# The last steps of a graph-attention layer on one core: products and selections placed earlier, row stores on two queues, scores by pairs with GpSimd

## The chip, the cores and the metric

One core of a Trainium2 chip. It has TensorE (PE), VectorE (DVE), ScalarE (ACT), GpSimd (POOL) and SyncE (SP), which only issues transfers here; ACT and POOL issue transfers too. The metric is the device time of one execution in microseconds (us), as the median of several. A "profiled execution" is one more execution, recorded by the hardware profiler: its span and all durations below come from it.

## The reference

A layer of attention over the edges of a graph, in front of it a layer norm and a relu, behind it a residual. There are N = 12,500 nodes of F = 128 features and E = 212,500 edges, sorted by the node `dst` that they end at; 8 heads of 16 features.

```python
h = jnp.maximum(_layernorm(x), 0.0)
q = (h @ Wq.T + bq).reshape(N, 8, 16)
k = (edge_h @ Wk.T + bk).reshape(-1, 8, 16)
v = (h @ Wv.T + bv).reshape(N, 8, 16)
qs, qd = q[src], q[dst]
in_m, out_m, diag_m = sum(qs * k), sum(qd * k), sum(qs * qd)   # over the 16 features
score = (softmax_of_dst(in_m / 4) + softmax_of_dst(out_m / 4)
         + softmax_of_dst(diag_m / 4)) * distance ** lam
h = segment_sum(score[..., None] * v[dst], dst, N).reshape(N, 128)
return x + leaky_relu(h @ Wo.T + bo, 0.1)
```

Since `v[dst]` is one row for all edges of a node, the last sum is v times one score per node and head: for each of the three softmaxes the kernel needs, per node and head, the sum of exp(logit) and the sum of exp(logit) times distance. Those are 24 + 24 numbers per node, called sums.

## The kernel before, in words

**Blocks and turns.** The edges are cut into blocks of 512. Five streams (S = 5) of 84 blocks (T = 84, G = 83) go side by side: step `g` of the loop handles stream `g % 5`, turn `t = g // 5`. There are 415 steps. In one step POOL issues four indirect transfers that gather q of the edges' sources (L683), PE transposes the edge rows and multiplies them by Wk (L1212, L1219, L1221) and spreads q of the ends (L1229), ACT builds one-hot matrices and copies out of PSUM (L1206, L1207, L1214, L1232), and DVE makes three products and a reduction to the logits (L1240 to L1243).

**Behind the logits**, a turn or two later, one call per step for all five streams: `turn_logits` transposes the logits into a PSUM tile `l_ps` (L1263); `scan_here` or, in the last turns, `scan_on` runs a maximum along the edges of a node forwards (L1321, with a short scan back over the block's head, L1326), and `scan_back` backwards (L1333); `turn_max` transposes that into `m_ps` (L1345); `powers` subtracts it on DVE (L1353) and takes the exponential on ACT (L1354, for the short piece behind the last turn L1358); `weigh_powers` multiplies by the distance's power (L1365). `select` loads the ends of the edges (L1371), `show_ends` compares them on PE into `d_ps` (L1379) and ACT makes 0/1 matrices of that (L1382, L1383). `to_rows` multiplies powers by these matrices into `w_ps` (L1393), 16 products a turn, copied by ACT (L1398), and `put_rows` stores the rows in DRAM as `sums`, five stores a turn (L1409); their places are register values, loaded into SP's registers once a turn (L654). The piece behind the last turn is called turn G (83) and has 16 partitions.

**Nodes.** Nodes are handled in units of 256 rows and pairs of units (class `Nodes`): load x and sums, normalise, multiply by Wv (`project_v`, bias L1150 and product L1152, into a PSUM tile that `weigh` reads), `scores` (L1094 to L1100: the two halves of the sums added, bounded below, a reciprocal, a product, two additions), `weigh` (v times score, L1160), `turn` (transposes L1144, ACT's copy L1147), `project_o` (bias L1150, product with Wo L1152, ACT's scaling by 0.1, L1171), `add_x` (the leaky relu's maximum, L1176, and the addition of x, L1177), `store` (L1183; the last part of the last unit L1185). Most pairs pass inside the loop, once their sums are complete. The pair called `leaving` has its product in the last turn; `last_pair` comes behind it; nine units are left to the end, as five pairs `rest[0]` to `rest[4]` (the last a single unit). Each of `rest`'s units has sums from one stream or from two; two parts are added (L1696). `hold(rest[r], name)` computes v of such a pair ahead and leaves it in a PSUM tile of that name.

**Order.** Each engine runs its instructions in the order of the program: every instruction is passed to `pin`, which chains it behind the last one of its engine. So a wait of one instruction holds all behind it on that engine. The PSUM tiles `l_ps`, `m_ps`, `d_ps`, `w_ps` and `node_ps` share three buffers (function `small`), handed out in the order of the program: a fourth waits until all readers of the first are done. `eT_ps` has one buffer, `k_ps` and `qd_ps` two each, shared with the loop.

Behind the loop the order was: the rest of turn 80's stores, logits and scans of turns 81 to 83, `powers` for all three, `weigh_powers` for all three, then `to_rows` and `put_rows` turn by turn; then the loads of all sums, the remaining `hold` products, the last pair's end, and the nine rest units:

```python
for r in range(len(rest) + 2):
    if r < len(rest):
        rest[r].weigh(rest[r].held)
    if 0 <= r - 1 < len(rest):
        rest[r - 1].turn(small([P, JN, P], "node_ps"))
    if 0 <= r - 2:
        rest[r - 2].project_o(small([P, JN, F], "node_ps"))
        rest[r - 2].add_x(nc.vector)
        rest[r - 2].store()
```

## Time and profile before

| what | value |
|---|---|
| median of 4 runs | 2201.59 us (2199.41 to 2204.81) |
| the profiled execution's own time | 2203.34 us |
| its span | 2201.5 us |
| instructions | 36,004 |
| busy PE, DVE, ACT, POOL | 1777.9, 2044.2, 1357.6, 1593.3 us |
| mean granted clock of PE | 0.792 |
| last gather issued by POOL (L683) | 2130.09 us |
| last reduction of logits on DVE (L1243) starts | 2135.81 us |
| last product of w_ps ends (L1393) | 2157.62 us |
| first load of the rest's sums on SP (L1125) | 2163.32 us |
| first weighing of a rest pair on DVE (L1160) | 2179.63 us |
| last store of the output issued (L1185) | 2195.08 us |

Times inside the execution count from the span's start. A row such as `L683 POOL DMA_INDIRECT qq<-q_table,src_i x1608 | 1526.7, 949 | 511.4` says: line 683, engine and operation, output and input tile, how often, then busy time, mean of one in ns, and the idle time in front of them. In a timeline a row is: start, duration, engine, line, operation, tiles and shapes, number of instructions run together, and in brackets how long the engine sat idle before it and what ended that. The granted clock says which share of its full clock PE was given: at 0.5 its instructions take twice as long.

### The profile page before, as it was taken

Reading aid. Unit: us, or ns where it says so; the run is one execution under the profiler, and the core shown is the slowest. Engines: PE = TensorE matmul, PEld = TensorE weight load, DVE = VectorE, ACT = ScalarE, POOL = GpSimd, SP = SyncE. Lnnn points to the kernel's source line nnn. Section 1 sums busy time; section 2 is a strip of 40 time slices with the busy share of each in tenths; the row PEclk is TensorE's granted clock in tenths of the full one; section 3 lists DMA queues with packets and bytes.
Section 4 is the critical chain, followed back from the end, with each engine's and each line's share of the span. In section 5 each row is a group of like instructions: output and inputs, shape, how many; then the busy total and the mean of one; then the engine's idle time right before and its main releaser. Section 6 shows DMA issues by size and latency. Waiting matters only on the chain.

```text
span 2201.5 us, 36004 instructions
## 1 busy us (share of the span) xinstructions
PE 1777.9 (81%) x10744; PEld 1415.4 (64%) x10744; DVE 2044.2 (93%) x2844; ACT 1357.6 (62%) x2518; POOL 1593.3 (72%) x1683
## 2 busy tenths in 40 slices
PE   6678788878888887887888887788887888778785
PEld 5556566656666666676676676666666677667664
DVE  7758999999999999999999999999999999999894
ACT  6665656656656665666566566566666566556561
POOL 7477777777777777777777777777777777777750
PEclk9766877887888888778778788787888787788776
DMA  7676554554555555545445545545545545544531
GB/s 213 202 227 176 178 159 149 180 170 149 184 161 163 153 180 184 162 145 183 150 145 176 163 147 161 170 143 161 173 140 176 163 144 167 161 152 142 160 95 58
DMA packets 321411, 355.63 MB, mean 162 GB/s; under 512 B 135267, under 2 KB 241006, under 8 KB 320897
## 3 DMA queue, kind: packets, MB, share of 16 engines
q1 hardware_dynamic: 250853, 237.91, 34.1%
q0 software_dynamic: 53184, 108.92, 17.3%
q10 hardware_dynamic: 17168, 6.41, 1.2%
q8 instruction: 87, 1.43, 0.3%
q14 instruction: 119, 0.97, 0.1%
HBM read 320.86 MB, written 32.17 MB: 160 GB/s over the span
## 4 chain that ended last, share of the span: by engine, by line
DVE 44%; PE 16%; DMA 13%; issue 4%; ACT 4%; POOL 2%; DVEq 1%; SPq 0%; ACTq 0%; POOLq 0%
DVE lT L1243 16%; DMA qq<-q_table,src_i 13%; DVE prod L1240 6%; DVE prod L1242 6%; DVE prod L1241 6%; PE k_ps L1221 4%; DVE m L1333 4%; PE w_ps L1393 3%; PE eT_ps L1212 3%; DVE l_ps L1303 2%; POOL qq L683 2%; PE k_ps L1219 1%; DVE back L1353 1%; PE m_ps L1345 1%; PE qd_ps L1229 1%
## 5 line engine op out<-in xcount | busy, mean ns | idle before, releaser
L683 POOL DMA_INDIRECT qq<-q_table,src_i x1608 | 1526.7, 949 | 511.4 <-issue 211.9
L1243 DVE TENSOR_REDUCE lT<-prod 128x96 f32<-128x1536 f32 x415 | 727.5, 1753 | 14.4
L1221 PEld LDWEIGHTS k_ps<-wk,eT 128*128 128x128 f32 x3320 | 502.8, 232 | 200.4 <-issue 200.4
L1221 PE MATMUL k_ps<-wk,eT 128*128 128x128 f32 x3320 | 594.1, 334 | 0.0
L1232 ACT COPY qd<-qd_ps 128x512 f32<-128x512 f32 x415 | 244.6, 589 | 153.3 <-DVE prod L1242 153.0
L1212 PE MATMUL eT_ps<-ident,ea 128*128 128x128 f32 x1660 | 312.0, 320 | 25.6 <-ACT eT L1214 24.6
L1354 ACT ACTIVATE back<-back 128x480 f32<-128x480 f32 x83 | 50.1, 604 | 423.3 <-DVE back L1353 417.9
L1206 ACT ACTIVATE relb<-relb,before 126x512 bf16<-126x512 bf16 x415 | 303.5, 731 | 0.0
L1240 DVE TENSOR_TENSOR prod<-qq,qd_ps 128x512 f32<-128x512 f32 x412 | 279.4, 678 | 25.0 <-ACT qd L1232 9.1
L1229 PE MATMUL qd_ps<-win,oh 126*128 126x128 bf16 x1660 | 190.2, 246 | 133.7 <-DVE prod L1240 109.2
L1214 ACT COPY eT<-eT_ps 128x512 f32<-128x512 f32 x415 | 239.8, 578 | 75.9 <-PE eT_ps L1212 59.5
L1242 DVE TENSOR_TENSOR prod<-qd,k_ps 128x512 f32<-128x512 f32 x415 | 282.5, 681 | 0.0
L1241 DVE TENSOR_TENSOR prod<-qq,k_ps 128x512 f32<-128x512 f32 x412 | 280.2, 680 | 0.0
L1212 PEld LDWEIGHTS eT_ps<-ident,ea 128*128 128x128 f32 x1660 | 233.0, 166 | 68.1 <-ACT eT L1214 47.2
L1207 ACT ACTIVATE oh<-relb 126x512 bf16<-126x512 bf16 x415 | 261.4, 630 | 14.3 <-DMA q_table<-q3o 1.2
L1229 PEld LDWEIGHTS <-oh 126*128 126x128 bf16 x1660 | 152.2, 112 | 158.2 <-issue 147.0
L1219 PE MATMUL k_ps<-b,ones 3*128 3x512 bf16 x415 | 185.3, 447 | 73.9 <-DVE prod L1242 73.3
L1393 PE MATMUL w_ps<-back,sel 128*126 128x144 f32 (+1 forms) x1344 | 213.9, 321 | 33.9 <-ACT sel L1383 18.0
L1393 PEld LDWEIGHTS w_ps<-back,sel 128*126 128x126 f32 (+1 forms) x1344 | 203.3, 220 | 41.0 <-ACT sel L1383 21.8
L1345 PE MATMUL m_ps<-ident,m 120*128 120x120 f32 x332 | 84.0, 402 | 86.4 <-DVE m L1333 83.3
L1345 PEld LDWEIGHTS m_ps<-ident,m 120*128 120x128 f32 x332 | 56.1, 216 | 105.5 <-DVE m L1333 70.4
L1333 DVE TENSOR_TENSOR_SCAN m<-far,head,l_ps 120x512 f32<-120x512 bf16 x81 | 103.0, 1271 | 0.0
(230 smaller groups left out, 1715.1 us busy)
## 6 DMA issues: line engine op xcount, KB each, us to landing
ea<-in_edge_attr_dram SPq DMA_DIRECT2D x83, 1280.0 KB
relb<-rel_d SPq DMA_DIRECT2D x83, 630.0 KB
qq<-q_table,src_i POOLq DMA_INDIRECT x1608
win<-q_table SPq DMA_DIRECT2D x415, 31.5 KB
far<-far_d SPq DMA_DIRECT2D x84, 120.2 KB
q_table<-q SPq DMA_DIRECT2D x18, 384.0 KB
sums<-rows SPq DMA_DIRECT2D x412, 7.9 KB
q_table<-xq SPq DMA_DIRECT2D x24, 256.0 KB
```

The lines of the kernel that those rows point to most:

```text
L683: rows = pin(nc.gpsimd.indirect_dma_start(out=qq[:, j, :], out_offset=None, in_=of, in_offset=bass.IndirectOffsetOnAxis(ap=at[:, s, j:j + ...
L1206: pin(nc.scalar.activation(d, d, AF.Abs, bias=before[:K3]))
L1207: pin(nc.scalar.activation(oh, d, AF.Relu, bias=1.0, scale=-1.0))
L1212: pin(nc.tensor.transpose(eT_ps[:, j, :], eas[g // S][:, g % S, j * F:(j + 1) * F], ident))
L1221: pin(nc.tensor.matmul(k_ps[:, j, :], eTs[g][:, j, :], wk, start=False, stop=(j == JN - 1)))
L1229: pin(nc.tensor.matmul(qd_ps[:, j, :], ohs[g][:, j * P:(j + 1) * P], d["win"][:, s, :], start=(j == 0), stop=(j == JN - 1)))
L1232: pin(nc.scalar.copy(qds[g], qd_ps))
L1240: pin(nc.vector.tensor_mul(prod[:, :, 1, :], qqs[g], q_ps[g]))
L1241: pin(nc.vector.tensor_mul(prod[:, :, 0, :], qqs[g], ks[g]))
L1242: pin(nc.vector.tensor_mul(prod[:, :, 2, :], qds[g], ks[g]))
L1243: pin(nc.vector.tensor_reduce(lTs[t][:, :, s, :], prod.rearrange("p j i (h d) -> p j (i h) d", d=DIM), AX.X, ALU.add))
L1393: pin(nc.tensor.matmul(w_ps[:, i].rearrange("p s c -> p (s c)"), d["sel"][:n, j, lo:lo + 3, :].rearrange("p s w -> p (s w)"), d["back"][:n ...
```

## The change

It touches the last three steps of the loop and what follows them.

- In the last turn `show_ends` of turn 80 moves from step 3 to step 2, that of 81 to step 3, those of 82 and 83 behind the last `turn_logits`. `hold(rest[0])` moves into step 3, `hold(rest[1])` and the last pair's `turn` into step 4, and `leaving.add_x` out of step 4.
- Behind the loop the last pair's Wv product comes after a `scan_back`; `powers`, `weigh_powers`, `to_rows` and `put_rows` go turn by turn, with the short turn's powers and rows in tiles of their own; stores of streams 3 and 4 of the last three turns are issued by ACT, whose registers get the places too; the leaving pair's additions and store, and the last pair's scores, come after the rows.
- Sums of a rest pair are loaded by one transfer per part instead of one per unit and part (`load_last`); the rest is sorted so that pairs are neighbours, both parts are loaded for both units of a pair (one more unit's sums are zeroed at the start), and POOL's memsets of `more` go.
- Scores are computed pair by pair; for all but `rest[0]` POOL adds the parts, the two halves and bounds them (`totals_of`). `leave` replaces `add_x` for the last pair and the rest: its maximum goes to SBUF and POOL adds x, except for the last unit.

```diff
         _, base_v[t] = nc.values_load_multi_w_load_instructions(
-            places[0:1, t, 0:S], engines=[mybir.EngineType.SP], min_val=0, max_val=N - 1,
+            places[0:1, t, 0:S], engines=[mybir.EngineType.SP] if t < G - 2 else
+            [mybir.EngineType.SP, mybir.EngineType.Activation], min_val=0, max_val=N - 1,
             skip_runtime_bounds_check_because="the indices of nodes are below N")
...
+    def totals_of(ab, engine):
+        den = ab[:, :, 0, 0:H3]
+        pin(engine.tensor_add(ab[:, :, 0, :], ab[:, :, 0, :], ab[:, :, 1, :]))
+        pin(engine.tensor_scalar(den, den, 1e-30, None, op0=ALU.max))
+
     def scores_of(ab, score):
-        pin(nc.vector.tensor_add(ab[:, :, 0, :], ab[:, :, 0, :], ab[:, :, 1, :]))
         den, num = ab[:, :, 0, 0:H3], ab[:, :, 0, H3:]
-        pin(nc.vector.tensor_scalar(den, den, 1e-30, None, op0=ALU.max))
         pin(nc.vector.reciprocal(den, den))
...
-        def load_sums(self, to=None, more=None):
-            self.ab = fin.tile([P, JN, 2, 2 * H3], F32, name="ab", bufs=3) if to is None else to
+        def load_sums(self):
+            self.ab = fin.tile([P, JN, 2, 2 * H3], F32, name="ab", bufs=3)
             for i, u in enumerate(self.of):
-                both = slice(2 * i, 2 * i + 2)
-                of = parts_of(u)
-
-                def rows(s):
-                    return (sums[s][u * UN:(u + 1) * UN].rearrange("(p k) i c -> p k (i c)", p=P))
-
-                pin(nc.sync.dma_start(self.ab[:, both].rearrange("p k i c -> p k (i c)"), rows(of[0])))
-                if len(of) > 1:
-                    pin(nc.scalar.dma_start(more[:, both].rearrange("p k i c -> p k (i c)"), rows(of[1])))
+                pin(nc.sync.dma_start(
+                    self.ab[:, 2 * i:2 * i + 2].rearrange("p k i c -> p k (i c)"),
+                    sums[parts_of(u)[0]][u * UN:(u + 1) * UN].rearrange("(p k) i c -> p k (i c)", p=P)))
+
+        def load_last(self, to, more):
+            self.ab, lo, n = to, self.of[0], len(self.of)
+            for q, to, s in zip((nc.sync, nc.scalar), (to, more), two_parts(self)):
+                pin(q.dma_start(
+                    to.rearrange("p (u k) i c -> p u (k i c)", k=2),
+                    sums[s][lo * UN:(lo + n) * UN].rearrange("(u p k) i c -> p u (k i c)", p=P, k=2)))
...
-        def scores(self):
+        def scores(self, totals=True):
             n = self.n
+            if totals:
+                totals_of(self.ab[:, :n], nc.vector)
             score = self.score = fin.tile([P, JN, HEADS], F32, name="score")
...
             pin(engine.tensor_add(y, to[:, :n], y))
+
+        def leave(self, to, engine):
+            n = self.n
+            self.product(to, bo3, wo)
+            o, y = self.h[:, :n], self.x[:, :n]
+            pin(nc.scalar.activation(o, to[:, :n], AF.Copy, scale=SLOPE))
+            pin(nc.vector.tensor_max(o, o, to[:, :n]))
+            pin(engine.tensor_add(y, o, y))
...
             pairs[t] = Nodes([todo.pop(0)[1], todo.pop(0)[1]])
-    rest = [u for _, u in todo] + [u for u in range(NU) if stored_at(u) is None]
+    rest = sorted([u for _, u in todo] + [u for u in range(NU) if stored_at(u) is None])
     rest = [Nodes(rest[i:i + 2]) for i in range(0, len(rest), 2)]
+
+    def two_parts(of):
+
+        return sorted({s for u in of.of for s in parts_of(u)})
+
+    assert all(len(two_parts(of)) < 3 and of.of[-1] - of.of[0] == len(of.of) - 1 for of in rest)
...
             d = st[t]
-            back = d["back"] = work.tile([P, JN, S, 2, H3], F32, name="back")
+            if t < G:
+                back = d["back"] = work.tile([P, JN, S, 2, H3], F32, name="back")
+            else:
+                back = work.tile([P, JN, 3, F], F32, name="prod", bufs=1)
+                back = d["back"] = back.rearrange("p j i f -> p (j i f)")[
+                    :, :JN * S * 4 * HEADS * 3 // 2].rearrange("p (j s i c) -> p j s i c", j=JN, s=S, i=2)
             mT = d["mT"].rearrange("p j (s c) -> p j s c", s=S)
...
                                          start=(i == 0 and j == 0), stop=(i == 1 and j == JN - 1)))
-            rows = work.tile([3 * W, 2, 3, 2 * H3], F32, name="rows")
+            if t < G:
+                rows = work.tile([3 * W, 2, 3, 2 * H3], F32, name="rows")
+            else:
+                rows = work.tile([P, JN, F], F32, name="qd").rearrange("p j f -> p (j f)")[
+                    :3 * W, :12 * H3].rearrange("p (i s c) -> p i s c", i=2, s=3)
             pin(nc.scalar.copy(rows, w_ps))
...
                     upto = 1 if t == T - 1 and s < S - 1 else W
-                    pin(nc.sync.dma_start(
+                    pin((nc.scalar if t > G - 3 and s > 2 else nc.sync).dma_start(
                         sums[s][first:NP][bass.ds(base_v[t][s], upto - first), t % 2, :],
...
                 old.project_o(small([P, JN, F], "node_ps"))
+            if t == G - 1 and s == 4:
+                hold(rest[1], "k_ps")
...
                 old.turn(small([P, JN, P], "node_ps"))
-            if old and even and s == 4:
+            if old and even and s == 4 and t < G - 1:
                 old.add_x(nc.vector)
+            if t == G - 1 and s == 3:
+                hold(rest[0], "eT_ps")
+            if t == G - 1 and s == 4:
+                new.turn(small([P, JN, P], "node_ps"))
             if old and not even and s == 0:
...
                     of.more = None
-                    if any(len(parts_of(u)) > 1 for u in of.of):
+                    if len(two_parts(of)) > 1:
                         more = gath.tile([P, JN, F], F32, name="qq").rearrange("p j f -> p (j f)")
...
                             "p (k i c) -> p k i c", k=of.n, i=2)
-                        pin(nc.gpsimd.memset(of.more, 0.0))
...
                 if t == G - 1:
+                    show_ends(t - 2)
                     turn_logits(t - 1)
...
             elif s == 3:
-                later(show_ends, t - 2)
+                if t < G - 1:
+                    later(show_ends, t - 2)
                 later(weigh_powers, t - 2)
...
                     select(G - 3 + s)
-                elif s == 4:
-                    for i in (G - 2, G - 1, G):
-                        show_ends(i)
+                if s == 3:
+                    show_ends(G - 2)
             behind[g + 1, 3] = pinned[products]
...
             if g < S:
-                of = [u for u in range(NU) if g in parts_of(u)]
+                of = [u for u in range(NU) if g in parts_of(u)
+                      or any(u in r.of and g in two_parts(r) for r in rest)]
                 pin(nc.scalar.dma_start(
...
         leaving, last_pair = pairs[G - 3], pairs[G - 1]
-        leaving.store()
         put_rows(G - 3, range(1, S))
         turn_logits(G - 1)
-        last_pair.scores()
-        last_pair.turn(small([P, JN, P], "node_ps"))
+        show_ends(G - 1)
+        show_ends(G)
         scan_on(G - 1)
-        hold(rest[0], "eT_ps")
-        last_pair.project_v(ps.tile([P, JN, F], F32, name="k_ps", bufs=2))
         scan_back(G - 2)
+        last_pair.project_v(ps.tile([P, JN, F], F32, name="qd_ps", bufs=2))
         turn_max(G - 2)
...
         turn_max(G - 1)
+        powers(G - 2)
         scan_back(G)
         turn_max(G)
-        for t in (G - 2, G - 1, G):
-            powers(t)
-        for t in (G - 2, G - 1, G):
-            weigh_powers(t)
+        powers(G - 1)
+        weigh_powers(G - 2)
+        powers(G)
+        to_rows(G - 2)
+        put_rows(G - 2)
+        weigh_powers(G - 1)
+        to_rows(G - 1)
+        put_rows(G - 1)
+        weigh_powers(G)
+        to_rows(G)
+        put_rows(G)
+        for r, of in enumerate(rest):
+            of.load_last(ends_ab[:, r * JN:r * JN + of.n], of.more)
+        leaving.add_x(nc.vector)
+        leaving.store()
+        last_pair.scores()
         last_pair.weigh(last_pair.held)
-        for t in (G - 2, G - 1, G):
-            to_rows(t)
-            put_rows(t)
+        hold(rest[2], "qd_ps")
+        hold(rest[3], "k_ps")
+        last_pair.turn(small([P, JN, P], "node_ps"))
+        hold(rest[4], "qd_ps")
+        last_pair.leave(small([P, JN, F], "node_ps"), nc.gpsimd)
+        last_pair.store()
         for r, of in enumerate(rest):
-            of.load_sums(ends_ab[:, r * JN:r * JN + of.n], of.more)
-        for r, name in ((1, "k_ps"), (2, "qd_ps"), (3, "qd_ps"), (4, "k_ps")):
-            hold(rest[r], name)
-        last_pair.turn(small([P, JN, P], "node_ps"))
-        last_pair.project_o(small([P, JN, F], "node_ps"))
-        last_pair.add_x(nc.vector)
-        last_pair.store()
-        ab = ends_ab[:, :sum(of.n for of in rest)]
-        for r, of in enumerate(rest):
+            engine = nc.gpsimd if r else nc.vector
             if of.more is not None:
-                some = ends_ab[:, r * JN:r * JN + of.n]
-                pin(nc.vector.tensor_add(some, some, of.more))
-        score = scan.tile([P, len(rest) * JN, HEADS], F32, name="end_score", bufs=1)
-        scores_of(ab, score[:, :ab.shape[1]])
-        for r, of in enumerate(rest):
-            of.score = score[:, r * JN:(r + 1) * JN]
+                pin(engine.tensor_add(of.ab, of.ab, of.more))
+            totals_of(of.ab, engine)
         for r in range(len(rest) + 2):
             if r < len(rest):
+                rest[r].scores(totals=False)
                 rest[r].weigh(rest[r].held)
...
             if 0 <= r - 2:
-                rest[r - 2].project_o(small([P, JN, F], "node_ps"))
-                rest[r - 2].add_x(nc.vector)
+                rest[r - 2].leave(small([P, JN, F], "node_ps"),
+                                  nc.vector if r - 2 == len(rest) - 1 else nc.gpsimd)
                 rest[r - 2].store()
```

## The prediction

> **What bounds the kernel now.** I read the page's busy times and costliest groups first, then the table of stretches, then the timelines of VectorE (DVE), SyncE (SP) and TensorE (PE) behind 2100 us, and the chain of waits for what ended each gap.
>
> ```profile
> PE 1777.9 (81%) x10744; PEld 1415.4 (64%) x10744; DVE 2044.2 (93%) x2844; ACT 1357.6 (62%) x2518; POOL 1593.3 (72%) x1683
> ...
> L683 POOL DMA_INDIRECT qq<-q_table,src_i x1608 | 1526.7, 949 | 511.4 <-issue 211.9
> ```
>
> GpSimd (POOL) issues 1,608 gathers of 0.949 us, with some 0.3 us between them; with DVE at 93% this paces the loop, about 25 us a turn. Up to step 412 of 415 the change leaves that alone, so some 2130 us cannot move. What can move is the end:
>
> ```profile
> 2120.00:2140.00 20.00, 15.80 (x68) 11.88 (x67) 19.76 (x25) 10.05 (x22) 10.00 (x13) 0.66 0.17 45
> 2140.00:2160.00 20.00, 17.65 (x99) 13.93 (x99) 9.31 (x17) 7.25 (x14) 0.00 (x0) 0.79 0.08 19
> 2160.00:2180.00 20.00, 9.23 (x35) 6.98 (x34) 9.15 (x13) 1.18 (x2) 0.00 (x0) 0.50 0.32 93
> 2180.00:2202.00 22.00, 11.44 (x59) 8.61 (x59) 8.76 (x15) 5.38 (x10) 0.00 (x0) 0.73 0.17 57
> ```
>
> Columns: stretch, its length, busy time of PE, weight loads, DVE, ACT, POOL, then PE's granted clock, DMA share and GB/s. DVE is full until 2140 and then under half busy; POOL is idle; no engine is the bound, a chain is. The clock is 0.50 for all of the third stretch, and that doubles PE's work there.
>
> ```profile
> 2135.81 1.75 DVE L1243 TENSOR_REDUCE lT<-prod 128x96 f32<-128x1536 f32 x1
> ...
> 2142.99 1.28 DVE L1321 TENSOR_TENSOR_SCAN u<-far,u,l_ps 120x512 f32<-120x512 bf16 x1 [2.06 <-PE l_ps L1263]
> ...
> 2149.18 1.22 DVE L1353 TENSOR_TENSOR back<-lT,m_ps 128x480 f32<-128x480 f32 x2 [1.27 <-PE m_ps L1345]
> ...
> 2170.57 0.70 DVE L1176 TENSOR_TENSOR node_ps<-h,node_ps 128x512 f32<-128x512 f32 x1 [15.19 <-ACT h L1171]
> ...
> 2175.41 2.85 DVE L1097 RECIPROCAL ends_ab<-ends_ab 128x432 f32<-128x432 f32 x1
> ...
> 2179.63 0.69 DVE L1160 TENSOR_TENSOR qq<-eT_ps,end_score 128x512 f32<-128x512 f32 x1
> ...
> 2185.61 0.70 DVE L1176 TENSOR_TENSOR node_ps<-qq,node_ps 128x512 f32<-128x512 f32 x1 [4.10 <-ACT qq L1171]
> ```
>
> These are the stations: last logits, last scan, first powers, last pair of the loop, scores of the nine rest units in one batch, their first weighing. The 15.19 us wait is the sums' way through DRAM:
>
> ```profile
> 2140.18 23.01 SPq L1409 DMA_DIRECT2D sums<-rows  x19
> 2163.32 5.71 SPq L1125 DMA_DIRECT2D ends_ab<-sums  x9
> ...
> 2195.08 0.27 SPq L1185 DMA_DIRECT2D out_dram<-qq  x1
> ```
>
> **Part by part.** The sum is made against the profiled execution, 2203.34 us, whose span is 2201.5; the last store is issued at 2195.08, and the 6.4 us behind it stay. The median is 1.75 us below that execution, and I carry the difference over.
>
> 1. Front, up to the end of the last w_ps product (2157.62). Removed: behind the last l_ps, PE did a turn, rest[0]'s product and the last pair's (2142.75 to 2148.68) before m_ps, so the powers came 6.19 us after the scan's start, while the scans themselves need 4.73 (2142.99 to 2147.72): 1.5 gained. The last l_ps also stood 3.7 us behind w_ps's end (2138.16 to 2141.84) because the selections' three PSUM buffers made PE wait for ACT; now l_ps comes first. Added: the products of rest[0] and rest[1] stand on PE in front of turn 80's w_ps and the last l_ps, 0.60 + 2.08 each at half clock, 5.4 in all, 2.9 at the full clock's 0.32 + 1.16; and turn 81's l_ps now needs a PSUM buffer that the powers (L1353) must read first, so scan_on(81), and the last two logits queued behind it on DVE, come 1.2 later. PE's idle 0.97 before w_ps swallows some. Half clock: 1.5 + 3.7 - 5.4 - 1.2 + 1.0 = -0.4. Full: +2.1, and it can't be more, since the logits themselves end 1.2 later. I take 0; the bounds are +2 and, if neither gain comes, -5.6.
>
> 2. Stores, loads, and the last pair (to 2170.57). Fifteen row stores at about 0.5 us, with a load of places of 1.33 between, kept SP until 2161.14; nine stay on SP and six go to ACT, which is idle but for three copies, so the last leaves about 1.2 earlier; the third rows copy has a buffer of its own now and no longer waits for stores (2.19 before). Places are now loaded on ACT also, 1.33 in its queue, before its stores of the last turn and nothing else. Loads: 16 become 9 (5 on SP, 4 on ACT), 5.71 becomes about 2.4, and rest[0] needs only its own: 2.56 landing after the first issue, near 2164.3. But on DVE the last pair's max (L1191 after) stands ahead of it, and its product waits on PE for rest[2], rest[3], a turn and rest[4]:
>
> ```profile
> 2157.77 1.44 PE L1152 MATMUL k_ps<-wv,qq 128*128 128x128 f32 x8
> 2159.14 0.60 PE L1150 MATMUL qd_ps<-b,ones 3*128 3x512 bf16 x1
> 2159.68 2.08 PE L1152 MATMUL qd_ps<-wv,qq 128*128 128x128 f32 x8
> ```
>
> Half clock: 2.68 x 3 + 1.06 + 1.6 + ACT's copy and scaling 1.3 = 12.0 behind 2157.62, 2169.6, 1.0 gained. Full: 6.9, 2164.5, 6.1 gained, and the loads are then as late. I take the middle, 3.5.
>
> Moved at no cost: the leaving pair's additions and the last pair's scores, 1.4 + 2.1 of DVE, go behind the rows into that 15.19 us wait; the leaving pair's two stores go on SP from before the row stores to behind the loads, where SP has 3 us with nothing due, and it keeps one small PSUM buffer until then. POOL's memsets (1.50, beside busy DVE) and two more zeroed columns at the start change nothing on the chain.
>
> 3. First scores. From that max to the first weighing DVE needed 9.06 (2170.57 to 2179.63): an addition of 0.69, four adds 1.96, a batch over 432 columns with a reciprocal of 2.85. Now: max 0.64, one add 0.5, and for one pair 0.35, 0.21, 0.75, 0.26, 0.19, 0.19 (the last pair's own at 2138.81 to 2140.93) with gaps, 3.2. Gain 5.9.
>
> 4. From first weighing to last store: 15.45. Each of the other pairs brings its scores back onto DVE, 0.75 + 0.26 + 0.19 + 0.19 and gaps, 1.5 x 3 + 1.0 = 5.5; the x additions that go to POOL free 0.69 x 4 = 2.8. DVE waited 5.56 for PE and ACT here (4.10 + 0.26 + 0.83 + 0.37), so part of 5.5 falls into that. Bounds: +0.4 and -2.7 (nothing covered); I take -1.8.
>
> 5. POOL beside DVE. POOL gets four adds, four totals, four max and four x additions. The trace has one meeting of the kind:
>
> ```profile
> 69.72 3.60 POOL L824 TENSOR_TENSOR step<-dst_r 104x2049 f32<-104x2049 f32 x1 [10.76 <-PE h_ps L908]
> ```
> ```profile
> 70.38 2.98 DVE L892 SCALAR_TENSOR_TENSOR shift<-sums,inv 128x14 f32<-128x14 f32 x1
> ```
>
> POOL's add costs 1.76 ns a column, so 0.68 for 384. DVE's L892, 0.17 elsewhere, took 2.98 and ended with POOL's. So a DVE operation with two inputs from SBUF waits out a POOL operation. Each pair has such operations on DVE (L1102 to L1104, and L1738 for the first): eight meetings at half of 0.65 are 2.6. Ends: 0, and all of POOL's adds and totals, 4 x 1.2 = 4.8.
>
> The Trainium skill, "SBUF — State Buffer", section "Who interferes with whom", speaks against this part: the port pair that DVE and GpSimd share is an exclusive lock, held for a whole instruction. It agrees with the 2.98 above; if the lock did not bind here, the sum would be 2.6 better.
>
> POOL's first max also has a library load in front of it, which before stood ahead of the first IOTA (POOL idle 0.40 there): 0 to 0.4, taken as hidden while DVE works on rest[0].
>
> The Trainium skill, "GPSIMD Engine Reference", section 2.1, gives about 6 us for the first call into a freshly loaded kernel; by it rest[1]'s totals would come some 4 us late, and the sum would be near 1. No row here shows that price.
>
> Sum: 0 + 3.5 + 5.9 - 1.8 - 2.6 = 5.0 gained. 2203.34 becomes 2198.3, the median 2201.59 becomes 2196.6.
>
> **The rivals.** (a) Forecast, 4.5 to 7.5 gained: 0.40. (b) Nothing that can be told. The middle of step 2 was generous: the clock stays at half as in 2158.5 to 2185.8, step 2 gives 1.0 and the meetings cost up to 4.8; gain 0 to 2.5, up to the 4.4 us of 0.2%, which is about what a measurement of this kernel can tell from no change: 0.32. For it: the 0.50 stretch above. Against it: fewer PE gaps. (c) More: PE gets the full clock, or POOL's work falls beside PE-bound waits: 0 + 6.1 + 5.9 - 1.8 - 0.5 = 9.7 gained, about 2192: 0.15. Against it: the 2.98. (d) Slower: PE's queue in front of w_ps at half clock. If PE still runs rest[0]'s and rest[1]'s products at half clock when turn 80's L1365 is done (2133.98), neither gain of step 1 comes, -5.6; PE, not the stores, then sets step 2, which gives 0; with 5.9 - 1.8 - 2.6 that is 4.1 lost, a median of 2205.7. It decides from w_ps starting 5 us late, beyond 2139. For it: the clock was half from 2124.4 to 2138.0. Against it: the idle 0.97, and the added products themselves keep PE busy, after which this trace went to full: 0.13.
>
> **How the numbers follow.** Most of (a) lies beyond 4.4 us, as all of (c): faster 0.53; (b) and the rest of (a): same 0.34; (d): slower 0.13. The range reaches from 2190.5, the good bounds of steps 2 to 5, to 2204, where (b) ends, with half of the measurement's own spread (5.4); it leaves out (d) and little of (c).
>
> **What would show it.** Right: the SP loads under 3 us; DVE's first weighing of a rest pair near 2172; 17 us and more from there to the last store, with DVE's reciprocals of 0.75 between; short DVE operations of 0.4 to 1 us in place of 0.2 beside POOL's. Step 1 is wrong if the last w_ps ends beyond 2160, step 2 if the last pair's max starts outside 2164 to 2170, step 5 if L1102 to L1104 stay at 0.2 to 0.26, and the library's price shows as a gap on POOL in front of L1097. The whole is wrong if the loop before 2130 moved.

## The result, and the profile after

The changed kernel takes 2205.86 us (median of 32 runs), the kernel before 2202.36 in the same comparison (52 runs): ratio 1.0014, interval 1.0009 to 1.0019. By the ratio it is 3.1 us slower, where 5.0 us faster was forecast, and lies above the range. The profiled execution took 2204.54 us with a span of 2202.7.

The table of stretches and the stations of DVE, as before the change:

```profile
2120.00:2140.00 20.00, 15.43 (x61) 10.35 (x61) 16.75 (x19) 9.54 (x20) 7.83 (x9) 0.58 0.15 41
2140.00:2160.00 20.00, 17.86 (x119) 14.76 (x119) 11.76 (x21) 7.50 (x14) 0.00 (x0) 0.91 0.04 6
2160.00:2180.00 20.00, 8.87 (x42) 6.63 (x40) 11.19 (x19) 2.90 (x5) 8.37 (x12) 0.61 0.36 111
2180.00:2203.00 23.00, 9.57 (x40) 6.60 (x38) 8.33 (x16) 3.77 (x8) 5.06 (x4) 0.57 0.17 55
```

```profile
2143.86 1.28 DVE L1342 TENSOR_TENSOR_SCAN u<-far,u,l_ps 120x512 f32<-120x512 bf16 x1 [5.78 <-PE l_ps L1284]
...
2166.07 0.69 DVE L1191 TENSOR_TENSOR h<-h,node_ps 128x512 f32<-128x512 f32 x1 [9.52 <-ACT h L1190]
...
2167.26 1.30 DVE L1096 TENSOR_TENSOR ends_ab<-ends_ab 128x192 f32<-128x192 f32 x1
2168.60 0.88 DVE L1097 TENSOR_SCALAR ends_ab<-ends_ab 128x96 f32<-128x96 f32 x1
2169.52 0.75 DVE L1101 RECIPROCAL ends_ab<-ends_ab 128x96 f32<-128x96 f32 x1
2170.30 0.26 DVE L1102 TENSOR_TENSOR ends_ab<-ends_ab 128x96 f32<-128x96 f32 x1
...
2170.82 0.94 DVE L1104 TENSOR_TENSOR score<-score,ends_ab 128x32 f32<-128x32 f32 x1
2171.80 0.69 DVE L1167 TENSOR_TENSOR qq<-eT_ps,score 128x512 f32<-128x512 f32 x1
```

The 15.19 us wait for the last pair has become 9.52, and the first weighing comes at 2171.80 instead of 2179.63. But three operations that take 0.35, 0.21 and 0.19 alone take 1.30, 0.88 and 0.94. The SP queue and POOL's last instruction of the program, then the closing instructions of POOL and SP (minimum, median, longest in ns, first and last start), the last two lines from the kernel before:

```profile
2160.26 2.88 SPq L1130 DMA_DIRECT2D ends_ab<-sums  x5
2164.38 4.81 SPq L1198 DMA_DIRECT2D out_dram<-x_in  x4
2182.15 11.53 SPq L1198 DMA_DIRECT2D out_dram<-qq  x8
2193.78 0.26 SPq L1200 DMA_DIRECT2D out_dram<-qq  x1
```
```profile
2191.08 1.26 POOL L1192 TENSOR_TENSOR qq<-qq 128x512 f32<-128x512 f32 x1 [2.06 <-DVE qq L1191]
```

```profile
L1764 POOLq INC_SWDGE_SEM  x1: 1579/1579/1579, 2194.5 to 2194.5; - x1
```
```profile
L1790 POOLq DRAIN  x3: 50/102/5789, 2196.1 to 2202.5; - x3
L1790 SPq DRAIN  x3: 7/7/13, 2199.0 to 2202.2; - x3
```
```profile
L1750 POOLq DRAIN  x3: 46/102/5777, 2136.4 to 2201.3; - x3
L1750 SPq DRAIN  x3: 7/7/13, 2200.7 to 2201.0; - x3
```

The last store leaves 1.30 us earlier than before (2193.78 against 2195.08), and yet the span is 1.2 us longer. Behind the program's last instruction every engine closes. SP's part ends at 2199.0 here. POOL's contains a drain of 5.79 us that starts at 2196.1 and ends at 2201.9, because POOL's last addition of x ended at 2192.34; before, the same drain ran from 2136.4, behind the gathers, where nobody waited for it, and SP's part, which ended at 2200.7, was the last. From the last store to the span's end it is 8.97 us now and was 6.47.

Executions differ by some 2 us in when the last gather is issued (2130.09 before, 2129.32 after; 2128.07 to 2130.44 in the first four experiments), so I count stations from there:

| station, us behind the last gather | before | after | gained | forecast |
|---|---|---|---|---|
| last w_ps product ends | 27.53 | 28.26 | -0.7 | 0 (step 1) |
| last pair's max | 40.48 | 36.75 | +4.5 more | +3.5 (step 2) |
| first weighing | 49.53 | 42.47 | +3.3 more | +5.9 (step 3) less a part of step 5 |
| last store issued | 64.99 | 64.46 | -6.5 more | -1.8 (step 4) less the other part |
| end of the span | 71.45 | 73.42 | -2.5 more | 0 |

Together 2.0 lost in these two profiles; the ratio of the medians says 3.1 (2.0 to 4.2).

### The profile page after: what moved, and what is told of

The parts are those of the page before. It is cut to its first block, busy times and chain, and to the rows that moved or that the text cites. A ratio compares the mean times of both kernels' runs of the same rounds, so it can differ in the third digit from the quotient of the medians.

```text
span 2202.7 us, 36027 instructions
## 1 busy us (share of the span) xinstructions
PE 1773.8 (81%) x10744; PEld 1410.0 (64%) x10744; DVE 2046.1 (93%) x2852; ACT 1358.4 (62%) x2518; POOL 1605.2 (73%) x1695
## 3 DMA queue, kind: packets, MB, share of 16 engines
q10 hardware_dynamic: 17786, 6.65, 1.2%
## 4 chain that ended last, share of the span: by engine, by line
DVE 50%; DMA 17%; PE 17%; issue 7%; ACT 4%; POOL 3%; DVEq 1%; ACTq 1%; SPq 0%; POOLq 0%
DVE lT L1264 18%; DMA qq<-q_table,src_i 16%; DVE prod L1261 7%; DVE prod L1263 7%; DVE prod L1262 6%; PE k_ps L1242 4%; DVE m L1354 4%; PE eT_ps L1233 3%; POOL qq L684 2%; DVE l_ps L1324 2%; PE w_ps L1419 2%; DVE back L1379 1%; PE k_ps L1240 1%; PE m_ps L1366 1%; PE qd_ps L1250 1%
## 5 line engine op out<-in xcount | busy, mean ns | idle before, releaser
L684 POOL DMA_INDIRECT qq<-q_table,src_i x1608 | 1526.5, 949 | 511.6 <-issue 218.6
L1419 PE MATMUL w_ps<-back,sel 128*126 128x144 f32 x1328 | 205.4, 315 | 30.8 <-ACT sel L1409 15.9
L1419 PEld LDWEIGHTS w_ps<-back,sel 128*126 128x126 f32 x1328 | 194.6, 214 | 37.5 <-ACT sel L1409 20.1
```

The costliest lines, as they stand in the source:

```text
L684: rows = pin(nc.gpsimd.indirect_dma_start(out=qq[:, j, :], out_offset=None, in_=of, in_offset=bass.IndirectOffsetOnAxis(ap=at[:, s, j:j + ...
L1419: pin(nc.tensor.matmul(w_ps[:, i].rearrange("p s c -> p (s c)"), d["sel"][:n, j, lo:lo + 3, :].rearrange("p s w -> p (s w)"), d["back"][:n ...
```

## The experiments

Ratios are against the kernel before, run beside each.

**The closing.** In the changed kernel only the last additions go back to DVE:

```diff
-                rest[r - 2].leave(small([P, JN, F], "node_ps"),
-                                  nc.vector if r - 2 == len(rest) - 1 else nc.gpsimd)
+                rest[r - 2].leave(small([P, JN, F], "node_ps"), nc.vector)
```

> The changed kernel, with the last addition of x of all rest pairs on DVE instead of POOL; POOL keeps the last pair's x and the totals, so its last instruction ends near 2176 instead of 2192.3. Theory A (POOL's closing ends the span: behind its last instruction come 1.7 us, then 1.58, then a drain of 5.79, 9.6 in all, against 5.3 from the last store to SP's end): the closing is off the path, the time from the last store's issue to the end of the span falls from 8.9 to 6.4 us; DVE takes 3 x 0.69 more, partly in its waits, so the time falls by 1 to 3 us against the changed kernel and comes to about the kernel before, ratio 0.9995 to 1.001. Rival B (the loss is all in DVE's scores by pairs and the meetings with POOL, the end is a constant of the program): 8.9 stays, and the time rises by 0 to 2 us.

And the kernel before gets one tiny late instruction on POOL:

```diff
+        late_pool = scan.tile([P, 8], F32, name="late_pool", bufs=1)
+        pin(nc.gpsimd.tensor_copy(late_pool, rest[-1].x[:, 0, 0:8]))
```

> The kernel before, plus one copy of 8 columns on POOL that waits for the last addition on DVE (the result goes nowhere). Theory A: POOL's closing starts at about 2194.5 instead of 2132.5 and ends near 2204.2 where SP's stood at 2200.7: 3 to 4 us slower, ratio 1.0014 to 1.0018, with a drain of about 5.8 us on POOL behind 2194. Rival B: one tiny instruction beside the last store costs nothing, ratio 1.000.

Measured: 1.0004 (0.9995 to 1.0012) and 1.0018 (1.0009 to 1.0027). The second is the sharp one: 188 ns of work, 4.0 us of time (2.0 to 6.0). The copy, and the drain behind it:

```profile
L1711 POOL COPY late_pool<-qq 128x8 f32<-128x8 f32 x1 | 0.2, 188 | 62.0 <-issue 62.0
```
```profile
L1752 POOLq DRAIN  x3: 46/102/5777, 2199.0 to 2205.4; - x3
```

From the last store to the end it is 12.61 us there. With the additions back on DVE it is 6.65. So the profiles show the closing in both directions: the last 2.5 us of the table are POOL's drain, started late. In the times only the late copy shows it clear of noise; the interval with the additions back on DVE touches that of the change.

**The meetings of POOL and DVE.** All of POOL's work behind the gathers goes to DVE:

```diff
-        last_pair.leave(small([P, JN, F], "node_ps"), nc.gpsimd)
+        last_pair.leave(small([P, JN, F], "node_ps"), nc.vector)
...
-            engine = nc.gpsimd if r else nc.vector
+            engine = nc.vector
...
+                rest[r - 2].leave(small([P, JN, F], "node_ps"), nc.vector)
```

> The changed kernel with everything that POOL does behind the loop on DVE (parts, totals and all additions of x). It prices the meetings of the two engines. If POOL's operations hold DVE up (L1096 1.30 for 0.35, L1097 0.88 for 0.21, L1104 0.94 for 0.19, L1102 0.92, 0.77 and 1.01 for 0.26, about 5 us in all), these go, 4 x 1.1 of adds and totals and 4 x 0.69 come to DVE, 7.2 in all, and the closing's 2.5 goes: within 1 us of the changed kernel. If DVE was not held up but slow for another reason, they stay, and it is 4 to 5 us slower than the changed kernel.

Measured: 0.9993 (0.9985 to 1.0002), better than both cases that I had written down: 0.21% or 4.6 us better than the change, each against the kernel before, with 7 us more work on DVE. The operations have their own lengths again:

```profile
2166.89 0.36 DVE L1096 TENSOR_TENSOR ends_ab<-ends_ab 128x192 f32<-128x192 f32 x1
2167.29 0.21 DVE L1097 TENSOR_SCALAR ends_ab<-ends_ab 128x96 f32<-128x96 f32 x1
...
2171.89 0.26 DVE L1102 TENSOR_TENSOR ends_ab<-ends_ab 128x96 f32<-128x96 f32 x1
```

From the first weighing to the last store it takes 18.81 us instead of 21.99. PE's clock in that stretch is 0.77 there instead of 0.58, so not all of this gain need be meetings. To price meetings without anything else, the kernel before gets additions on POOL that nobody reads, beside its batch:

```diff
+        idle = scan.tile([P, 4 * 4 * H3], F32, name="idle", bufs=1)
+        for of in rest:
+            if of.more is not None:
+                some = of.more.rearrange("p k i c -> p (k i c)")
+                for _ in range(3):
+                    pin(nc.gpsimd.tensor_add(idle[:, :some.shape[1]], some, some))
```

> The kernel before, plus twelve additions of 384 columns on POOL, three behind the landing of each second part, reading that part and writing a tile that nobody reads; no instruction of another engine waits for them, and POOL's closing ends long before the span. It prices the meetings alone. If a DVE operation with two inputs from SBUF waits out POOL's (about 1.0 us each): L1696, L1094 and L1098 to L1100 grow by 0.3 to 1 us each, the reciprocal (2.85) and the operations that read PSUM do not, 2 to 5 us in all, ratio 1.001 to 1.002. If they do not disturb each other: the same durations as before and 1.000.

Measured: 1.0014 (1.0005 to 1.0023). DVE's timeline:

```profile
2169.30 4.35 DVE L1702 TENSOR_TENSOR ends_ab<-ends_ab,qq 128x384 f32<-128x384 f32 x4
2173.68 1.57 DVE L1094 TENSOR_TENSOR ends_ab<-ends_ab 128x864 f32<-128x864 f32 x1
2175.28 0.38 DVE L1096 TENSOR_SCALAR ends_ab<-ends_ab 128x432 f32<-128x432 f32 x1
2175.70 2.85 DVE L1097 RECIPROCAL ends_ab<-ends_ab 128x432 f32<-128x432 f32 x1
```

Four adds took 1.96 and now take 4.35, the next 1.57 for 1.06; POOL's last addition ends at 2174.34, and behind it all is as before. 2.9 us of DVE, 3.1 us of time (1.1 to 5.1).

**The front.** The changed kernel with the last turn in its old order, up to the powers:

```diff
-            if t == G - 1 and s == 4:
-                hold(rest[1], "k_ps")
...
-            if t == G - 1 and s == 3:
-                hold(rest[0], "eT_ps")
-            if t == G - 1 and s == 4:
-                new.turn(small([P, JN, P], "node_ps"))
...
+                elif s == 4:
+                    for i in (G - 2, G - 1, G):
+                        show_ends(i)
...
-        last_pair.project_v(ps.tile([P, JN, F], F32, name="qd_ps", bufs=2))
+        last_pair.project_v(ps.tile([P, JN, F], F32, name="k_ps", bufs=2))
```

> The changed kernel with the order of the kernel before in the last turn and up to the powers (selections in step 4, products of rest 0 and 1, the leaving pair's additions and the last pair's turn at their old places). If the front is as it seems in the two profiles (last product of w_ps ends 0.7 us later after the last gather than before): the time falls by 0 to 1.5 us, while rest 1's product comes behind w_ps and gives back up to 1.5. If moving the front was a gain that something else hid, it rises by 2 us or more.

Measured: 1.0017 (1.0008 to 1.0025). Within the noise that is the change's own 1.0014, so the front is neutral: step 1's 0 holds, and rival (d) falls. The condition of (d) was met (in the changed kernel w_ps of turn 80 starts at 2140.56, 6.4 later than before, beyond 2139), but those 16 products then ran at the full clock, 2.12 us instead of 4.10, and the last l_ps came soon behind them:

```profile
2140.56 2.12 PE L1419 MATMUL w_ps<-back,sel 128*126 128x144 f32 x16
2142.52 0.60 PE L1151 MATMUL node_ps<-ident,h 128*128 128x128 f32 x4
2143.17 0.66 PE L1284 MATMUL l_ps<-ident,lT 128*120 128x128 f32 x4
```

**Stores and loads alone.** Old front, changed stores, loads and row order, the old batch on DVE (the loop over `rest` is the one of the kernel before, with `project_o` and `add_x`):

```diff
-        last_pair.leave(small([P, JN, F], "node_ps"), nc.gpsimd)
+        last_pair.project_o(small([P, JN, F], "node_ps"))
+        last_pair.add_x(nc.vector)
...
+        totals_of(ab, nc.vector)
+        scores_of(ab, score[:, :ab.shape[1]])
```

> Of the change only the front end's back half (powers to rows turn by turn, third rows copy in a buffer of its own), the row stores on two queues and the shared loads; the last turn's order, the one batch of scores on DVE and the additions of x are as in the kernel before, POOL does nothing behind its gathers. Theory A (the stores and loads were a gain of 3.7 to 4.9 us, seen at the last pair's max, and the scores by pairs lost it again: 22.0 us from the first weighing to the last store for 15.4): max at 35.6 us behind the last gather, weighing 9.1 later, last store 15.4 later, at 60.1 against 65.0, end 6.4 later: ratio to the kernel before 0.9975 to 0.9985. Rival B (the batch only moved the wait: loads that come earlier are not what the batch waits for): last store at 63 to 65, ratio 0.9993 to 1.0003.

Measured: 0.9998 (0.9988 to 1.0007): my theory expected 0.9975 to 0.9985 and falls; the earlier stores and loads gained nothing in this kernel. The last pair's max came 39.91 us behind the last gather, not 35.6: the loads were issued (the last at 32.78, in the kernel before at 38.50), but PE was not done. The 8 us behind the last w_ps product, in this kernel and in the changed one:

```profile
2157.15:2165.15 8.00, 8.00 (x33) 6.08 (x33) 0.00 (x0) 0.40 (x1) 0.00 (x0) 0.55 0.51 151
```
```profile
2157.62:2165.62 8.00, 5.95 (x36) 4.49 (x35) 0.00 (x0) 1.16 (x3) 0.00 (x0) 0.91 0.55 161
```

PE is busy for all of the first, at a clock of 0.55; with the changed front, which also leaves less work there, it is done early at 0.91.

PE is only one of two things that the last pair waits for. On ACT, the issues of the second parts' loads stand in front of the copy of the last pair's turn. In the kernel before PE ended that turn at 2166.62 and ACT the issues at 2167.15, almost together. Two other kernels happened to have PE at its full clock in these 8 us: first the one with the late copy on POOL, which has the old loads, then the changed kernel with the old front, which has the new ones:

```profile
2160.84 0.60 PE L1144 MATMUL node_ps<-ident,h 128*128 128x128 f32 x4
2161.34 4.56 ACTq L1127 DMA_DIRECT2D qq<-sums  x7
2165.95 0.59 ACT L1147 COPY hT<-node_ps 128x512 f32<-128x512 f32 x1 [9.03 <-DMA qq<-sums]
```
```profile
2161.30 2.25 ACTq L1130 DMA_DIRECT2D qq<-sums  x4
2162.90 0.60 PE L1151 MATMUL node_ps<-ident,h 128*128 128x128 f32 x4
2163.59 0.59 ACT L1154 COPY hT<-node_ps 128x512 f32<-128x512 f32 x1 [5.06 <-PE node_ps L1151]
```

In the first PE is done with the turn at 2161.44 and the copy waits for the issues. From the last w_ps product to the last pair's max it is 12.95 us in the kernel before, 13.29 with the full clock alone, 12.42 with the new stores and loads alone, and 7.97 with both (one profile each). So neither gains much alone, and together they gain 5.0 us.

Which clock comes is partly the order's doing. With the changed front all nine profiles, of six kernels, had 0.79 to 0.93 in these 8 us; with the old one three profiles had 1.00 and seven, the kernel before among them, 0.55 to 0.57. To see this I ran the changed front with the batch, and second profiles:

> The changed front, stores and loads with the batch of scores of the kernel before. With the old front the same end had the last pair's max at 39.9 us and the ratio 0.9998; the changed kernel has it at 36.8. If the order of PE's work decides the clock there: max at 36 to 37.5, weighing 9.1 and last store 24.5 later, near 61.5, ratio 0.9980 to 0.9988. If the clock there is chance: 0.9995 to 1.0003.

> A second profile of the kernel with the old front and the batch: in the first PE had half its clock from 2157 to 2170 and the last pair's max came 39.9 us behind the last gather, while the variant with the old front and scores by pairs, the same instructions up to there, had full clock and 35.6. If the clock is chance, this one may show either; if it is set by the instructions, 39 to 40 again.

> A second profile of the changed kernel. If the stations of the first are typical: last w_ps product 28 to 29 us, last pair's max 36.5 to 37.5, first weighing 42 to 43 and last store 64 to 65 us behind the last gather, POOL's drain 5.8 us and the last 2 to 3 us of the span behind SP's end.

In these runs, the next one and the two that close this section the kernel before itself took 2740 us. In the changed kernel POOL's idle time between gathers was 935.8 us instead of 511.6; what made the loop slower is open (two expectations speak of another chip, but the record gives these runs the same chip number as the seven experiments before them). So only ratios and stations behind w_ps count. From the last w_ps product the batch with the old front needed 12.52 us to the last pair's max (12.42 in its first profile), with the changed front 7.94; the changed kernel 7.95 (8.49 in its first). Its drain again ended 3.0 us behind SP's part, and from its first weighing to its last store it took 20.86 us at a clock of 0.72, after 21.99 at 0.58. Ratio of the changed front with the batch: 0.9990 (0.9982 to 0.9999), in a second set 0.9994 (0.9981 to 1.0006), where the last pair's max came after 8.31 us:

> The changed front with the batch once more. On the other chip its last pair's max came 8.0 us behind the end of the w_ps products, as in the changed kernel (8.5), while with the old front it was 12.5 in both profiles. If that holds, max at 36 to 37.5 us behind the last gather, last store near 61, ratio 0.9978 to 0.9990, clearly below the 0.9998 of the old front with the batch. If the clock is chance, 12 us and 0.9995 to 1.0003.

The max came early in both, as the order of PE's work would have it; both ratios lie between what I had written for that and what for chance, and neither differs from the 0.9998 of the old front beyond the noise.

**Idle work for PE.** Four unread products behind the last pair's, in the changed kernel (n is 4):

```diff
+            for _ in range(n):
+                to = small([P, JN, F], "node_ps")
+                last_pair.product(to, bo3, wo)
```

> The changed kernel with four products of 128x512 on PE that nobody reads, in the 7.2 us that PE waits behind the last pair's product (some 1.5 us each). It asks whether the half clock from 2174.7 to 2191.8 costs the pairs' end, and whether PE's wait brings it. If so: clock 1.0 for most of the stretch from the first weighing to the last store, product rows of 1.16 instead of 2.08, turns of 0.63 instead of 1.06, and with 1.4 us less for each of the pairs that DVE waits on (2.3 and 2.6 us waits) the last store comes 3 to 5 us earlier and the ratio to the kernel before is 0.9990 to 1.0003. If DVE and POOL set the end, the clock rises and the time falls by under 1 us: 1.001 to 1.0015. If the idle work does not move the clock, nothing changes.

Measured: 1.0010 (1.0001 to 1.0019). The clock from the first weighing to the last store rose from 0.58 to 0.70, the stretch fell from 21.99 to 21.45 only: it is DVE and POOL that mostly set the pace there.

**Rest 0 ahead.** DVE idles for 9.5 us in front of the last pair's max. With the old front, rest 0 is scored there, the others in one batch, none on POOL:

```diff
+        score_rest([0])
+        rest[0].weigh(rest[0].held)
+        last_pair.add_x(nc.vector)
+        last_pair.store()
+        rest[0].turn(small([P, JN, P], "node_ps"))
+        rest[0].project_o(small([P, JN, F], "node_ps"))
+        score_rest(list(range(1, len(rest))))
```

> The kernel of the batch, but rest 0 is scored and weighed by itself on DVE in front of the last pair's max (DVE idle for 10 us there), turned and multiplied behind the last pair's product, and the other four pairs are scored in one batch. If the loads of rest 0 have landed by 33 us behind the last gather, its 3.2 us of DVE lie in the idle time, the batch shrinks by 1.7 us and one pair's turn and product (1.9 to 3.7 us of PE) leave the end: 2 to 4 us better than the batch alone, ratio 0.996 to 0.9975. If the sums land later than 35, it pushes the last pair's max back and gains under 1 us.

> The kernel with rest 0 ahead and one batch for the others, with three unread products of 128x512 on PE in its wait for the batch. If the granted clock follows PE's load, the four pairs behind the batch run at the full clock: up to 1.4 us less for each pair that PE holds, 1 to 3 us better than without. If the clock is full there anyhow, or the wait too long for three products, within 0.5 us.

> The kernel with rest 0 ahead, the other pairs scored in two batches (1 and 2, then 3 and 4, the second behind the weighing of 2) instead of one. The first batch takes about 1.2 + 0.55 + 0.25 + 1.5 + 0.35 + 0.2 + 0.2 = 4.2 us instead of 6.2, so PE gets rest 1 some 2 us sooner; DVE pays about 0.7 more in all, while it waited 3.8 and 1.5 us for PE in the one batch. If PE at the head of the four pairs sets the end: 1 to 2 us better than rest 0 ahead alone (0.9976 to 0.9982). If DVE does, or if PE falls to the lower clock for longer because its work is spread: 0 to 1 us worse.

> The same with every pair scored by itself, all on DVE, none on POOL: the changed kernel's pairs without its meetings and its closing. Theory (pairs cost DVE more instructions and leave PE idle in between): DVE needs 1.0 us more than with two batches and PE's clock stays low, 1 to 2 us worse than the one batch, ratio 0.999 to 0.9995. Rival (pairs are right, only POOL was wrong): as good as or better than batches, 0.998 or less.

Measured, in this order: 0.9985 (0.9976 to 0.9994), with idle products 0.9982 (0.9973 to 0.9991), two batches of two 0.9983 (0.9974 to 0.9992), each pair by itself on DVE 0.9993 (0.9984 to 1.0002). The first three beat the kernel before by 3 to 4 us (of the first I had expected more, 0.996 to 0.9975) and can't be told apart; pairs one by one seem to lose 2 us of it, though the intervals touch.

```profile
2163.80 0.56 DVE L1732 TENSOR_TENSOR ends_ab<-ends_ab,qq 128x384 f32<-128x384 f32 x1 [9.29 <-DMA qq<-sums]
...
2166.56 0.69 DVE L1167 TENSOR_TENSOR qq<-eT_ps,end_score 128x512 f32<-128x512 f32 x1
2167.17 0.69 DVE L1183 TENSOR_TENSOR node_ps<-h,node_ps 128x512 f32<-128x512 f32 x1
```

These rows are from the first of the four. Here DVE waits for the sums (9.29, DMA), no longer for PE. Whether this order would gain as much with the old loads was not run.

> The changed kernel's whole front, stores and loads, behind them the end that did best so far: rest 0 scored on DVE ahead of the last pair's max, the others in two batches, nothing on POOL. If the changed front is neutral: as with the old front, 0.9978 to 0.9988. If the products moved ahead keep PE at the full clock from 2158 to 2166 (the changed kernel and two of its variants show 36.8 to 37.4 us to the last pair's max), the wait for the sums sets it anyhow and nothing is gained; if they delay the scans as in the variant with POOL's additions on DVE (16.0 instead of 12.9), it is 1 to 2 us worse.

> The kernel with the changed front and rest 0 ahead once more, since the runs before were on a chip on which the kernel before itself takes 2739.8 us. There the ratio was 0.9990, some 2.7 us less. If the gain is one of microseconds at the end, it is the same 2 to 4 us here: 0.9982 to 0.9990; if the old front was better, the ratio lies above the 0.9983 of the old front with the same end.

The changed front with rest 0 ahead and two batches of two: 0.9990 (0.9980 to 0.9999) and 1.0001 (0.9990 to 1.0012), both worse than I had expected for a neutral front. It is no better than the old front; whether worse can't be said across the two conditions.

## Why the prediction was wrong

The prediction's signs of being right all came: SP's loads took 2.88 us, the first weighing started at 2171.80, and it took 21.99 us to the last store with reciprocals of 0.75 between. But none of them looked behind the last store, and "17 us and more" had no upper end. Rival (d) named 2205.7, close to the median of 2205.86, but by accident: its path, PE's queue in front of w_ps, was not the one that lost the time.

**The premise of the sum failed:** "the last store is issued at 2195.08, and the 6.4 us behind it stay". I costed POOL's new work by its instructions and never asked what follows POOL's last one. The trace of before shows the answer, 1.59 and 5.78 us in POOL's closing instructions at 2134.7 and 2136.4, hidden then. It costs 2.5 us here and was no term and no rival.

**Step 5 was right in its mechanism and half of its size.** Forecast 2.6, ends 0 to 4.8. The prolonged operations add up to (1.30 - 0.35) + (0.88 - 0.21) + (0.94 - 0.19) + (0.92 - 0.26) + (0.56 - 0.19) + (0.77 - 0.26) + (1.01 - 0.20) + (0.60 - 0.42) = 4.9, just beyond the upper end. The change's second profile repeats the first seven of these. There are eight, as forecast, and together they are 0.55 of the POOL operations beside them, near the half that I took. What I mis-sized were those operations: 1.45, 1.10, 0.99, 0.99, 0.59, 1.27, 1.26 and 1.26 us, 1.11 on average, not 0.65. POOL's addition of 384 columns took 0.99 to 1.10 us, not the 0.68 of 1.76 ns a column; and four of the eight meet additions of x, of 512 columns (POOL has five of these, where I counted four). The Trainium skill, "SBUF — State Buffer", section "Who interferes with whom", has the port pair that the two engines share as an exclusive lock; the additions beside the batch agree (4.35 us for 1.96). The reciprocal of the change kept its 0.75 beside POOL's L1096.

**Step 3** was right but for these meetings: 9.06 became 5.72; less the 2.4 of L1096, L1097 and L1104 that is 3.4, forecast 3.2.

**Step 4 was mis-sized.** Forecast -1.8, bounds +0.4 to -2.7; measured -6.5, of which 2.5 are meetings. My -1.8 let DVE's waits for PE and ACT absorb 0.9 of the scores' 5.5. They came to 2.31 + 0.68 + 2.64 + 0.57 = 6.2 instead of 5.56, so they absorbed nothing, with PE's clock at 0.58 instead of 0.80 in that stretch. By DVE's rows the 6.5 are 4.9 more busy time (9.13 became 14.04: the 2.5 of meetings, and 2.4 of scores less x, forecast 2.7), 0.6 more waits, and 0.55 more from DVE's last operation to the last store's issue; the rest is small gaps. In front of that issue SP has the stores of the pair before, whose x POOL added until 2192.34. With nothing on POOL the stretch is 18.81, 3.4 more than the batch's 15.45. What the clock has of the waits no run separates; at 0.70 (idle products) and 0.72 (the change's second profile) the whole stretch was 21.45 and 20.86.

**Step 2** came out at 4.5 for 3.5. Its two ends were right in kind: 1.0 at half clock and 6.1 at the full clock, for which the old front with the new loads shows 0.5 and 5.0. That the middle came near is luck: PE had 0.91 of its clock here, which I had not forecast, and the changed front left it less work.

**The library load** shows no price: L1096 on POOL ends at 2170.08 and the first max (L1097) starts at 2170.18. The first two rows are operations of POOL that step 5 meets.

```profile
2166.90 1.45 POOL L1192 TENSOR_TENSOR x_in<-h,x_in 128x512 f32<-128x512 f32 x1 [36.63 <-DMA qq<-sums]
2168.31 1.10 POOL L1738 TENSOR_TENSOR ends_ab<-ends_ab,qq 128x384 f32<-128x384 f32 x1
2169.49 0.59 POOL L1096 TENSOR_TENSOR ends_ab<-ends_ab 128x192 f32<-128x192 f32 x1
2170.18 0.47 POOL L1097 TENSOR_SCALAR ends_ab<-ends_ab 128x96 f32<-128x96 f32 x1
2170.72 0.99 POOL L1738 TENSOR_TENSOR ends_ab<-ends_ab,qq 128x384 f32<-128x384 f32 x1
```

The 6 us of the Trainium skill, "GPSIMD Engine Reference", section 2.1, do not show; the gap is 0.1, and the measurement decides.

So in the changed kernel's 3.1 us, POOL's use costs 4.6 (1.0014 against 0.9993). About half of it went when only the last additions left POOL (1.0014 to 1.0004, though the intervals touch), which is mostly the closing; the other half I put down to the meetings, but PE's clock differed too (0.77 for 0.58) and is not separated. What remains of the change gains 1.5, which its interval does not tell from nothing.

## What to carry to other kernels

Before giving an idle engine work near the end, look up in the trace how long that engine takes to close and when it starts to; a short instruction there can cost more than the work that it relieves. Small DVE operations beside GpSimd's additions are priced by GpSimd's durations, not by their own. And ask whether a wait has two causes that end almost together: the earlier loads gained 0.5 us while PE was slow, a fast PE gained nothing while the loads were late, and both together gained 5.0.

## What the runs showed of the hardware that I had not expected

POOL's closing took 9.6 us from the end of its last instruction in the kernel before and in the change, and 9.3 to 11.5 us in the profiles of the experiments (11.5 behind the late copy). Two instructions in it hardly vary, 1.58 and 5.78 us, whether POOL had only gathered or also computed. DVE's TENSOR_SCALAR with one input from SBUF is held up by POOL's addition too (0.88 for 0.21), its reciprocal is not (0.75). And not every POOL operation holds DVE up: L1102 at 2170.30, with two inputs from SBUF, kept its 0.26 beside POOL's TENSOR_SCALAR of 2170.18 to 2170.65, and so in all five profiles in which POOL adds up the totals. With the changed order of the last turn PE had 0.79 to 0.93 of its clock in the 8 us behind the last w_ps product, nine times of nine; with the old order 0.55 to 0.57 seven times and 1.00 three times. What decides it no run shows.
